# Layer 0 of a two-layer Fourier attention kernel: another opening, and transforms of 128 columns

## The chip, the cores and the metric

The kernel runs on one core of a Trainium2 chip. The core has a matrix engine (TensorE, PE in the profile, with its weight loads as PEld), VectorE (DVE), ScalarE (ACT), GpSimd (POOL) and SyncE (SP), which here only issues transfers. Each engine works through its own instructions in order and waits on semaphores for the others. The metric is the device time of one execution in microseconds, and lower is better. Everything is float32.

## The reference, cut to what matters

The input is four batches of 32 images of 128x128. Layer 0 normalises them (per group of image columns, then per image) and takes a Fourier transform of each image, of which 64 row and 33 column frequencies ("modes") are kept. Three sets of spectral weights make keys, queries and values for 32 heads. Attention runs over the 32 images of a batch, head by head, and the result is projected back. Two more spectral layers with a GELU between them follow, with a residual:

```python
xn = _inorm(xa, norm1_w, norm1_b)
k = _fno_layer(xn, Kcw, Ksw, Hs, Ws)
q = _fno_layer(xn, Qcw, Qsw, Hs, Ws)
v = _fno_layer(xn, Vcw, Vsw, H, W)
...
scores = jnp.einsum('bntk,bnsk->bnts', qf, kf) / (np.float32(np.sqrt(Hs * Ws)) * temperature)
p_attn = jax.nn.softmax(scores, axis=-1)
...
m = _fno_layer(an, m0cw, m0sw, H, W, inner_norm=True, act=True)
m = _fno_layer(m, m1cw, m1sw, H, W, inner_norm=True, act=False)
out = _inorm(m, mon_w, mon_b) + a
```

Layer 1 is an additive attention over the tokens and a mixture of experts. The change does not touch it.

## The kernel before

The kernel never forms keys, queries or values as images. All of it is done on modes. A mode is a pair of frequencies; with real and imaginary part, 64 row frequencies fill the 128 partitions.

A Tile scheduler sets the order of each engine's instructions from the program's order and its own estimates of time, and puts in the semaphores. A tile with the same tag and one buffer (`bufs=1`) reuses its memory, so a new writer waits for the last reader of the old contents. Pools of PSUM tiles have two buffers per tag.

**Loads.** `load(b)` (L113) brings a batch of images in as four transfers of 512 KB, two on SP's queue and two on ScalarE's. Then constants come on SP's queue (`cst`, `icol`, `par`). The spectral weights of the two later layers (`mcw_raw`, `mcol`, L153 to L159), `hs`, `pv` and `psw2` (L194 to L201) come as thirteen small transfers on ScalarE's queue. `mcw_raw` has one buffer for two sets, so the second set's transfer waits until VectorE has copied the first. ScalarE's table of functions is loaded in `logarithms()` (L299), which stands behind them.

**Statistics.** `image_sums` (L314) squares the images on ScalarE (L320), sums images and squares over rows with TensorE (`rows`, L324), copies the sums out (`ev`, L332) and turns them (`s12`, L337). A chain of small operations on VectorE, ScalarE and TensorE follows: `sv`, `mg`, `gm`, `gn_r` (the reciprocal deviation of a group), `colg` (the column transform scaled by it), `my`, `n_r` and `n_s` (the scale of each image).

**Key and query weights.** `padded` (L394) loads a weight with heads on 32 partitions, pads it from 32 to 64 row frequencies and makes its first column symmetric. For K and Q the kernel then multiplies on 32 partitions (L429 to L435), and brings the products to modes on partitions with 34 transposes on TensorE (L441). `w_re` and `w_im` are the result.

**Images' spectra.** `spectra_of_images` (L459) calls `forward` (L266) for groups of eight images. `forward` multiplies an image by `rows`, 192 columns wide: cosine, negative sine, negative cosine (`pz`, L274, two images to a PSUM tile). `evacuate` copies it to `z`, two calls in three on ScalarE (L219), the third on VectorE (L221). Two matmuls an image (`px`, L281 and L282) take the first 128 and the last 128 columns of `z` as weights. The results go to `xx`. The later layers' `spectra(0, q)` and `spectra(1, gl)` call the same `forward`. After all groups `xx` is corrected in places and written to a DRAM scratch `xd` with two transfers (L487), from where `xb` is read back in broadcast form (L698).

**Value weights.** `value_weights` (L500) multiplies value and projection weights on 32 partitions, writes them to DRAM (`gd`) and reads them back in broadcast (`gb`). It is called after the images' spectra.

**Attention.** `attention_weights` (L524) forms products over pairs of images on VectorE (`pa`) and GpSimd (`pb`), contracts them with `w_re` and `w_im` on TensorE (`sp`), adds the skip path and takes the softmax. The probabilities go through DRAM (`prd`) to `pr`. In the loop over batches `xb` is copied (`xw`, L707), multiplied with `gb` (`u`, L713 and L715) and contracted with `pr` (`po`, L718). For batches 1 to 3 the same work of the next batch is spread into the batch before it.

In the loop, between the first layer's spectra and the GELU, stands a chain on VectorE: `sqx` (L810), `v_s` (L814), `r0`, `hq` (L828). `add_attention` (L770), 32 updates of `x` a batch, may run anywhere between the attention's scale and the end of the batch.

Of the kernel before, what the change touches and what calls it, by code (L numbers as in the profile page):

```python
# [7 lines left out]
F32 = mybir.dt.float32  # L8
# [5 lines left out]
P = 128  # L14
# [21 lines left out]
def _constants():  # L36

    w = np.arange(P)
    kx = np.concatenate([np.arange(32), np.arange(-32, 0)])
    ky = np.arange(KY)  # L40
    th = 2 * np.pi / P
    c, s = np.cos(th * np.outer(w, kx)), np.sin(th * np.outer(w, kx))
    rows = np.concatenate([c, -s, -c], 1)
    inv_rows = np.concatenate([c.T, -s.T], 0)
    angle = th * np.outer(w, ky)
    cc, cs = np.cos(angle), np.sin(angle)

    cols1 = np.concatenate([cc[:, 32:33], cs, cc, -cs], 1) / NPIX
    cols2 = np.concatenate([0 * cc[:, :1], -cc, cs, cc], 1) / NPIX
    twice = np.where(ky == 0, 1.0, 2.0)[:, None]  # L50
    re, im = twice * cc.T, -twice * cs.T
    inv_cols = np.concatenate([re, im], 0)
    p = np.arange(P)
    same = (p[:, None] % 32 == np.arange(32)[None, :]).astype(np.float64)
    block = (p[:, None] // 32 == np.arange(4)[None, :]).astype(np.float64)

    eye = np.eye(32)
    comb = np.zeros((4, 32, 3, 32))
    comb[0, :, 0], comb[3, :, 0] = eye, -eye
    comb[1, :, 1], comb[2, :, 1] = eye, eye  # L60
    comb[:, :, 2] = -comb[:, :, 0]
    halves = np.concatenate([np.eye(64), np.eye(64)], 0)

    group = (p[:, None] // 4 == p[None, :] // 4) / (4.0 * NPIX / C * T)
    of_group = p[:, None] // 4 == np.arange(32)[None, :]
    by_p = np.concatenate(
        [rows, inv_rows, cols1, cols2, same, block, comb.reshape(P, 96), halves, group, of_group / 4],
        1,
    )
    return by_p.astype(np.float32), inv_cols.astype(np.float32)  # L70
# [3 lines left out]
NCONST = 192 + 128 + 2 * NX + 32 + 4 + 96 + 64 + P + 32  # L74
# [30 lines left out]
def layer0(  # L105
    tc, x, kcw, qcw, vcw, pcw, m0cw, m1cw, mcol0, heads, small_row, by_p, inv_cols, dram, x1
# [12 lines left out]

    loaded = load(0)  # L120
# [12 lines left out]
    rows = columns(192)  # L133
# [17 lines left out]

    mcw, energy, cross = [], [], []
    for n, src in enumerate((m0cw, m1cw)):  # L153
        t = const.tile([P, KY, 2], F32, name=f"mcw{n}_raw", tag="mcw_raw")
        m = const.tile([P, 2], F32, name=f"mcol{n}")
        for half in range(2):
            rows_h = slice(half * KX, (half + 1) * KX)
            nc.scalar.dma_start(out=t[rows_h], in_=src)
            nc.scalar.dma_start(out=m[rows_h], in_=mcol0[n])  # L159
        w = const.tile([P, 2, KY], F32, name=f"mcw{n}")  # L160
        nc.vector.tensor_copy(w, t.rearrange("p y r -> p r y"))
        mcw.append(w)
        sq = const.tile([P, 2, KY], F32, name=f"msq{n}")
        nc.vector.tensor_mul(sq, w, w)
        en = const.tile([P, KY], F32, name=f"energy{n}")
        nc.vector.tensor_tensor(en, sq[:, 0], sq[:, 1], ALU.add)
        lone = const.tile([P, 1], F32, name=f"lone{n}")
        nc.vector.tensor_scalar(lone, en[:, 0:1], 0.5, None, ALU.mult)
        nc.vector.tensor_scalar(en, en, 2.0, None, ALU.mult)

        h = const.tile([P, 2], F32, name=f"hermitian{n}")
        nc.vector.tensor_tensor(h[:, 0:1], w[:, 0, 0:1], m[:, 0:1], ALU.add)
        nc.vector.tensor_tensor(h[:, 1:2], w[:, 1, 0:1], m[:, 1:2], ALU.subtract)
        nc.vector.tensor_scalar(h, h, 0.5, None, ALU.mult)
        cr = const.tile([P, KY], F32, name=f"cross{n}")
        nc.vector.tensor_scalar(cr, w[:, 0], 2.0, None, ALU.mult)
        nc.vector.tensor_copy(cr[:, 0:1], h[:, 0:1])
        nc.vector.tensor_mul(h, h, h)
        nc.vector.tensor_tensor(en[:, 0:1], h[:, 0:1], h[:, 1:2], ALU.add)
        for r in (0, 64):  # L180
            nc.vector.tensor_copy(en[r + 32 : r + 33, 0:1], lone[r + 32 : r + 33])
            for v in (en, cr):
                nc.vector.memset(v[r : r + 1, 0:1], 0.0)
        energy.append(en)
        cross.append(cr)


# [6 lines left out]
    nc.scalar.dma_start(out=hs, in_=heads)  # L194
    ks, qs, vs, psw = (hs[:, i : i + 1] for i in range(4))
    pv = const.tile([2 * NH, 1], F32, name="pv")
    nc.scalar.dma_start(out=pv[:NH], in_=heads[:, 2:3])
    nc.scalar.dma_start(out=pv[NH:], in_=heads[:, 2:3])
    psw2 = const.tile([2 * NH, 1], F32, name="psw2")
    nc.scalar.dma_start(out=psw2[:NH], in_=heads[:, 3:4])  # L200
    nc.scalar.dma_start(out=psw2[NH:], in_=heads[:, 3:4])  # L201
    nc.vector.tensor_mul(pv, pv, psw2)

# [11 lines left out]
    def evacuate(out, in_):  # L215

        flip[0] = (flip[0] + 1) % 3
        if flip[0]:
            nc.scalar.copy(out, in_)  # L219
        else:  # L220
            nc.vector.tensor_copy(out, in_)  # L221
# [44 lines left out]
    def forward(images, c1, c2, take, change=None):  # L266
# [4 lines left out]
        for k in range(0, GI, 2):  # L271
            pz = ps.tile([P, 2, 192], F32, name="pz", tag="a")
            for j in range(2):
                nc.tensor.matmul(pz[:, j], images[k + j], rows, start=True, stop=True)  # L274
            evacuate(z[:, k : k + 2], pz)
# [23 lines left out]
    def logarithms():  # L299
        tc.keep_in_program_order(nc.scalar.preload_act_table_set("natural_log_exp_and_others"))  # L300

    logarithms()
# [86 lines left out]
    normed = image_sums(0, loaded)  # L389

# [3 lines left out]
    def padded(src, name, tag):  # L394
        raw = prep.tile([NH, 32, KA, 2], F32, name=f"{name}_raw", tag="raw", bufs=2)
# [17 lines left out]

    k_re, k_im = padded(kcw, "k", "k")
    q_re, q_im = padded(qcw, "q", "q")
    nc.vector.tensor_scalar(k_re, k_re, ks, None, ALU.add)
    nc.vector.tensor_scalar(q_re, q_re, qs, None, ALU.add)


    t1 = prep.tile([NH, KX, KA], F32, name="t1")  # L420
    t2 = prep.tile([NH, KX, KA], F32, name="t2")
    wd = prep.tile([NH, KA, 2, KX], F32, name="wd", tag="wd")
    for part, (a, b, c, d, op) in enumerate(
        (
            (q_re, k_re, q_im, k_im, ALU.add),
            (q_im, k_re, q_re, k_im, ALU.subtract),
        )
    ):
        nc.vector.tensor_mul(t1, a, b)  # L429
        nc.vector.tensor_mul(t2, c, d)  # L430
        nc.vector.tensor_tensor(t1, t1, t2, op)
        for half in range(2):
            view = wd[:, :, half, :].rearrange("n y x -> n x y")
            nc.vector.tensor_scalar(view, t1, 128.0, None, ALU.mult)
        nc.vector.tensor_scalar(wd[:, 0], wd[:, 0], 0.5, None, ALU.mult)  # L435
        dst = (w_re, w_im)[part]
        for y0 in range(0, KA, 16):
            n = min(16, KA - y0)
            pt = ps.tile([P, 16, NH], F32, name="pt", tag="a")
            for y in range(n):  # L440
                nc.tensor.transpose(  # L441
                    pt[:, y, :],
                    wd[:, y0 + y].rearrange("n h x -> n (h x)"),
                    ident[:NH, :NH],
                )
            nc.vector.tensor_copy(dst[:, y0 : y0 + n], pt[:, :n])

    nc.vector.memset(w_re[96:97, 0], 0.0)
    qk1 = prep.tile([NH, 1], F32, name="qk1")
    nc.vector.tensor_scalar(qk1, qs, ks, 128.0, ALU.mult, ALU.mult)  # L450
    qkd = prep.tile([NH, NH], F32, name="qkd")
    nc.vector.tensor_scalar(qkd, ident[:NH, :NH], qk1, None, ALU.mult)
    ones_n = prep.tile([NH, NH], F32, name="ones_n")
    nc.vector.memset(ones_n, 1.0)
    pq = ps.tile([NH, NH], F32, name="pq", tag="a")
    nc.tensor.matmul(pq, ones_n, qkd, start=True, stop=True)
    nc.vector.tensor_copy(qk, pq)

    def spectra_of_images(b, xt, normed):  # L459
# [4 lines left out]
        xx = modes.tile([P, T, n], F32, name=f"xx_{b}", tag="xx")  # L464
        for g in GROUPS:
# [12 lines left out]


        nc.vector.tensor_copy(xx[0:1, :, 1 + KY], par[0:1, N1B : N1B + 1].to_broadcast([1, T]))  # L480
        nc.vector.tensor_copy(xx[64:65, :, 1], par[64:65, N1B : N1B + 1].to_broadcast([1, T]))
# [3 lines left out]
        xd = dram.tile([T, 2, KX, KY], F32, name=f"xd_{b}")  # L485
        for part in range(2):
            nc.sync.dma_start(  # L487
                out=xd[:, part].rearrange("t x y -> x t y"),
                in_=xx[64 * part : 64 * part + 64, :, 1 + KY :],
            )  # L490
# [9 lines left out]
    def value_weights():  # L500

# [116 lines left out]

    front = spectra_of_images(0, loaded, normed)
    value_weights()  # L620
# [861 lines left out]
```

## Time and profile before

| | us |
|---|---|
| median of 3 runs (lowest, highest) | 3248.1 (3234.64, 3252.51) |
| the profiled execution | 3246.97 |
| its span | 3245.1 |
| PE, DVE, ACT, POOL busy | 3004.3, 2324.5, 2327.1, 2138.9 |
| granted TensorE clock, mean | 0.967 |

Some points of time in the profiled execution, from the timeline, for batch 0: the first `rows` matmul starts at 6.19 and the first square at 20.61; `gn_r` is done at 42.4 and `n_s` at 56.4; the copies `xm` of the finished spectra start at 76.26; the first product `pa` starts at 79.44; the first `po` starts at 125.61; `py`, which follows the last `po`, starts at 193.77.

The views: the *page* gives busy time and the costliest groups of instructions, with the idle time just before them and what ended most of it. The *chain of waits* follows the work that ended last back to what released each step. The *timeline* lists instructions in order. *Stretches* give the busy time of each engine between two moments. A float32 matmul appears as two records in the trace, so 256 records of `pz` are 128 images.

### The profile page before, as it was taken

How to read it: one execution, taken by the hardware profiler on the slowest of the kernel's cores; microseconds unless marked ns; L12 is line 12 of the kernel's file. 1: busy time of each engine (PE TensorE's matmuls, PEld its weight loads, DVE VectorE, ACT ScalarE, POOL GpSimd, SP SyncE). 2: the span in 40 equal slices, each digit the busy share in tenths (PEclk: the TensorE clock that was granted, in tenths of full speed). 3: DMA queues.
4: the chain of work that ended last, by engine and by line, in shares of the span. 5: the costliest groups of instructions: out<-in, count | busy, mean ns of one | idle time of the engine just before them, and what ended most of it. 6: DMA issues, size and time to landing. Idle time of an engine off the chain costs nothing.

```text
span 3245.1 us, 53386 instructions
## 1 busy us (share of the span) xinstructions
PE 3004.3 (93%) x19732; PEld 1584.7 (49%) x19732; DVE 2324.5 (72%) x5070; ACT 2327.1 (72%) x3205; POOL 2138.9 (66%) x1883
## 2 busy tenths in 40 slices
PE   6899899899898789999999999999999999999997
PEld 4378458548657734443444444444444435444443
DVE  6776767777686456777765868876677777687787
ACT  2244344354353469999998999998999999899992
POOL 1631551460461259978789887979878889888773
PEclk9899899999999779999999999999999999999999
DMA  4410420340230121010110010011100010101000
GB/s 107 111 32 1 100 70 1 50 121 1 29 116 1 44 55 30 1 37 7 25 42 23 1 36 14 8 30 30 30 14 24 14 36 24 36 1 30 14 14 13
DMA packets 150853, 111.67 MB, mean 34 GB/s; under 512 B 35870, under 2 KB 139393, under 8 KB 149985
## 3 DMA queue, kind: packets, MB, share of 16 engines
q1 hardware_dynamic: 133873, 102.42, 12.6%
q10 hardware_dynamic: 16720, 5.84, 0.8%
q8 instruction: 156, 2.56, 0.3%
q14 instruction: 104, 0.85, 0.1%
HBM read 67.26 MB, written 20.00 MB: 27 GB/s over the span
## 4 chain that ended last, share of the span: by engine, by line
PE 65%; POOL 10%; ACT 9%; DVE 8%; issue 6%; DMA 2%; ACTq 0%; POOLq 0%; DVEq 0%; SPq 0%
PE d L1293 19%; PE po L1312 11%; PE px L1181 6%; ACT r L1346 4%; PE po L718 4%; PE pz L274 4%; PE n L1293 4%; PE four L296 3%; POOL e L1355 3%; PE pv L291 3%; PE px L282 2%; PE px L281 2%; POOL e L1354 2%; ACT e L1362 2%; PE sk L682 1%
## 5 line engine op out<-in xcount | busy, mean ns | idle before, releaser
L1351 DVE TENSOR_TENSOR r<-n,r 128x1024 f32<-128x1024 f32 (+1 forms) x1056 | 961.4, 952 | 481.9 <-PE n L1293 388.5
L1354 POOL TENSOR_TENSOR e<-r 128x512 f32<-128x512 f32 x528 | 673.2, 1275 | 269.2 <-DVE r L1351 268.9
L1346 ACT ACTIVATE r<-d 128x1024 f32<-128x1024 f32 (+1 forms) x1056 | 793.0, 802 | 66.7 <-PE n L1293 59.9
L1358 ACT ACTIVATE r<-r 128x1536 f32<-128x1536 f32 x528 | 783.5, 1484 | 16.7
L1355 POOL TENSOR_TENSOR e<-e,r 128x512 f32<-128x512 f32 x528 | 671.5, 1272 | 41.4
L1293 PE MATMUL d<-qe,ke 32*128 32x512 f32 (+3 forms) x2304 | 611.0, 605 | 38.2 <-ACT r L1346 36.3
L1293 PE MATMUL n<-qe,ke 32*128 32x512 f32 (+3 forms) x2304 | 608.4, 603 | 0.0
L1312 PE MATMUL po<-e,kx 128*128 128x512 f32 (+3 forms) x1152 | 594.7, 605 | 13.4 <-POOL e L1367 13.4
L1293 PE MATMUL d<-qf,kf 32*128 32x512 f32 (+3 forms) x2304 | 555.2, 556 | 0.0
L1293 PE MATMUL n<-qf,kf 32*128 32x512 f32 (+3 forms) x2304 | 555.0, 556 | 0.0
L1185 DVE SCALAR_TENSOR_TENSOR xc<-px,wgt,xc 128x128 f32<-128x128 f32 x1024 | 358.1, 350 | 40.5 <-PE px L1181 9.5
L1362 ACT ACTIVATE e<-e 128x512 f32<-128x512 f32 x528 | 325.7, 617 | 64.4 <-POOL e L1355 63.7
L1312 PEld LDWEIGHTS po<-e,kx 128*128 128x128 f32 x1152 | 175.7, 188 | 392.2 <-issue 310.2
L1293 PEld LDWEIGHTS d<-qe,ke 32*128 32x128 f32 x2304 | 177.6, 184 | 360.1 <-ACT r L1346 340.8
L800 POOL TENSOR_TENSOR spec<-spec,part 128x264 f32<-128x264 f32 x64 | 55.5, 867 | 392.7 <-DVE part L797 188.9
L713 POOL TENSOR_TENSOR u<-xb,gb 128x858 f32<-128x858 f32 (+1 forms) x120 | 234.7, 1981 | 119.0 <-PE po L718 102.5
L1293 PEld LDWEIGHTS d<-qf,kf 32*128 32x128 f32 x2304 | 221.8, 187 | 177.1 <-issue 164.5
L1181 PE MATMUL px<-we,x2t 128*128 128x512 f32 x512 | 264.9, 603 | 6.8 <-DVE xc L1185 6.0
L715 DVE TENSOR_TENSOR u<-xw,gb 128x858 f32<-128x858 f32 (+1 forms) x200 | 206.6, 1084 | 51.1 <-PE po L718 37.1
L1293 PEld LDWEIGHTS n<-qf,kf 32*128 32x128 f32 x2304 | 229.0, 186 | 20.0 <-issue 12.4
L718 PE MATMUL po<-u,pr 128*32 128x429 f32 (+1 forms) x1280 | 188.6, 542 | 18.4 <-POOL u L713 8.8
L1293 PEld LDWEIGHTS n<-qe,ke 32*128 32x128 f32 x2304 | 178.0, 183 | 9.8 <-DVE r L1351 0.9
(369 smaller groups left out, 4254.4 us busy)
## 6 DMA issues: line engine op xcount, KB each, us to landing
xb<-xd SPq DMA_DIRECT2D x128, 214.5 KB
xc<-x SPq DMA_DIRECT2D x31, 512.0 KB
x<-x SPq DMA_DIRECT2D x16, 512.0 KB
qf<-qe SPq DMA_DIRECT2D x64, 128.0 KB
out<-xc SPq DMA_DIRECT2D x15, 512.0 KB
xb<-xd SPq DMA_DIRECT2D x32, 198.0 KB
gb<-gd SPq DMA_DIRECT2D x4, 1056.0 KB
x<-in_x ACTq DMA_DIRECT2D x8, 512.0 KB
```

Source lines behind the costliest of these rows:

```text
L713: nc.gpsimd.tensor_tensor(u, xb, gk, ALU.mult)
L718: nc.tensor.matmul(po[32 * j : 32 * j + 32], pr[:, i, k], u[:, r], start=i == 0 and k == 0, stop=i == 3 and k == 1,)
L1181: nc.tensor.matmul(px, x2t[:, k * P : (k + 1) * P], we[:, e0 : e0 + 4], start=True, stop=True)
L1185: nc.vector.scalar_tensor_tensor(xc[:, k], px[:, e], wgt[:, k, e0 + e : e0 + e + 1], xc[:, k], ALU.mult, ALU.add)
L1293: nc.tensor.matmul(o, k, q, start=turn == 0 or g > 0, stop=turn == 1 or g > 0)
L1312: nc.tensor.matmul(sums[c, h][:, q0 : q0 + c1 - c0], kx[:, jb], e[:, c0:c1], start=jb == 0, stop=is_last and q0 > 2 * P, skip_group_check= ...
L1346: nc.scalar.activation(r[:, g], d, AF.Ln, scale=1.0 / DSCALE)
L1351: nc.vector.tensor_tensor(r[:, g], part, r[:, g], ALU.mult)
L1354: nc.gpsimd.tensor_tensor(e, r[:, 1], r[:, 2], ALU.add)
L1355: nc.gpsimd.tensor_tensor(e, e, r[:, 0], ALU.add)
L1358: nc.scalar.activation(r, r, AF.Exp, scale=-1.0)
L1362: nc.scalar.activation(e, e, AF.Exp)
```

## The change

It has six parts.

- The table load (`logarithms()`) moves to the front, before `load(0)`. All small loads move from ScalarE's queue to SP's, and those of the later layers' weights, with the VectorE work on them, behind the key and query weights.
- `value_weights()` is called first, before `image_sums`. Its temporaries `t1`, `t2` are its own, and `padded` has one buffer for the raw weight instead of two.
- Key and query weights are laid out by the host with modes on partitions (`kq_modes`, `kq_mirror`, `heads_row`). They are loaded to both halves of the partitions and multiplied there as 128x544, without padding and without transposes.
- `rows` has 128 columns, without the negative cosine. `pz` holds four images, and the third block of `z` is made by a second evacuation with the sign changed.
- `evacuate` takes a sign: `activation(Copy, scale)` on ScalarE instead of `copy`, `tensor_scalar` on VectorE instead of `tensor_copy`, for all its callers.
- The bias of `xx` and the write to `xd` are done for each group of eight images, two small copies and two transfers of 66 KB each time.

```diff
-    rows = np.concatenate([c, -s, -c], 1)
+    rows = np.concatenate([c, -s], 1)
...
+    logarithms()
     loaded = load(0)
...
-    rows = columns(192)
+    rows = columns(128)
...
-            nc.scalar.dma_start(out=t[rows_h], in_=src)
-            nc.scalar.dma_start(out=m[rows_h], in_=mcol0[n])
...
-    nc.scalar.dma_start(out=hs, in_=heads)
+    nc.sync.dma_start(out=hs, in_=heads)
...
-    def evacuate(out, in_):
+    def evacuate(out, in_, sign=1.0):
         flip[0] = (flip[0] + 1) % 3
         if flip[0]:
-            nc.scalar.copy(out, in_)
+            nc.scalar.activation(out, in_, AF.Copy, scale=sign)
         else:
-            nc.vector.tensor_copy(out, in_)
+            nc.vector.tensor_scalar(out, in_, sign, None, ALU.mult)
...
-        for k in range(0, GI, 2):
-            pz = ps.tile([P, 2, 192], F32, name="pz", tag="a")
-            for j in range(2):
+        for k in range(0, GI, 4):
+            pz = ps.tile([P, 4, P], F32, name="pz", tag="a")
+            for j in range(4):
                 nc.tensor.matmul(pz[:, j], images[k + j], rows, start=True, stop=True)
-            evacuate(z[:, k : k + 2], pz)
+            evacuate(z[:, k : k + 4, :P], pz)
+            evacuate(z[:, k : k + 4, P:], pz[:, :, :64], -1.0)
...
-    k_re, k_im = padded(kcw, "k", "k")
-    q_re, q_im = padded(qcw, "q", "q")
...
-            for y in range(n):
-                nc.tensor.transpose(
-                    pt[:, y, :],
-                    wd[:, y0 + y].rearrange("n h x -> n (h x)"),
-                    ident[:NH, :NH],
-                )
-            nc.vector.tensor_copy(dst[:, y0 : y0 + n], pt[:, :n])
...
+            for r, y in ((0, 1 + KY), (64, 1)):
+                bias = par[r : r + 1, N1B : N1B + 1].to_broadcast([1, GI])
+                nc.vector.tensor_copy(xx[r : r + 1, i, y], bias)
+            for part in range(2):
+                nc.sync.dma_start(
+                    out=xd[i, part].rearrange("t x y -> x t y"),
+                    in_=xx[64 * part : 64 * part + 64, i, 1 + KY :],
+                )
...
+    value_weights()
+    normed = image_sums(0, loaded)
     front = spectra_of_images(0, loaded, normed)
-    value_weights()
...
+    nc.sync.dma_start(out=skip, in_=heads_row[: 2 * NH].partition_broadcast(P))
...
+        for h in range(2):
+            r = slice(64 * h, 64 * h + 64)
+            nc.sync.dma_start(out=raw[r], in_=kq_modes[n])
+            nc.sync.dma_start(out=rev[r], in_=kq_mirror[n])
...
+    for dst, a, c, op in (
+        (w_re, q_re, q_im, ALU.add),
+        (w_im, q_im, q_re, ALU.subtract),
+    ):
+        t = prep.tile(shape, F32, name="wt", tag="wt")
+        nc.vector.scalar_tensor_tensor(dst, a, 128.0, k_re, ALU.mult, ALU.mult)
+        nc.vector.scalar_tensor_tensor(t, c, 128.0, k_im, ALU.mult, ALU.mult)
+        nc.vector.tensor_tensor(dst, dst, t, op)
+        nc.vector.tensor_scalar(dst[:, 0], dst[:, 0], 0.5, None, ALU.mult)
...
+            nc.sync.dma_start(out=t[rows_h], in_=src)
+            nc.sync.dma_start(out=m[rows_h], in_=mcol0[n])
```

## The prediction

> **What bounds the kernel now.** I read the span first: 3245.1 us, inside an execution of 3246.97. Layer 1 begins at about 1128 us and the change does not touch it, so some 2117 us stay. Then the chain of waits over the first 130 us. Columns: start us, us, what.
>
> ```profile
> 4.91 7.48 DMA mcw_raw<-in_m0cw
> 13.35 6.09 DMA mcw_raw<-in_m1cw
> ...
> 35.65 1.19 DVE t L431
> ...
> 76.98 15.32 DMA xd<-xx
> 92.32 16.41 DMA xb<-xd
> ```
>
> Two tiny loads hold the first 19 us, VectorE's K/Q products on 32 partitions hold 24 to 42, then the transforms, then a scratch write and its read-back up to 109. The timeline says how the tiny loads get there: they stand on ScalarE's queue ahead of its table load and the squares, and one of them waits for a buffer.
>
> ```profile
> 19.31 1.28 ACT L300 ACT_TABLE_LOAD   x1 [19.31 <-DMA mcw_raw<-in_m1cw]
> 20.61 1.06 ACT L320 ACTIVATE xx<-x 128x1024 f32<-128x1024 f32 x1
> ...
> 30.56 0.58 ACT L332 COPY ev<-rows 64x512 f32<-64x512 f32 x1 [6.06 <-PE rows L324]
> ```
>
> The image was there at 6.2 us (the first `rows` matmul runs at 6.19), the squares start at 20.61, the sums end at 30.5. Third, the groups, for the transforms of all four batches (busy, mean ns | idle before):
>
> ```profile
> L219 ACT COPY z<-pz 128x384 f32<-128x384 f32 x127 | 60.5, 477 | 120.2 <-PE pz L274 119.9
> L274 PE MATMUL pz<-cst,x 128*128 128x192 f32 x256 | 54.3, 354 | 4.0 <-ACT z L219 3.0 <-DVE z L221 1.0
> L282 PE MATMUL px<-colg,z 128*128 128x67 f32 x256 | 49.1, 275 | 0.0
> ```
>
> ScalarE waits for TensorE (120 us), TensorE hardly for ScalarE (3): these stages are bound by TensorE. `pz` alone is 3.9% of the whole chain, 127 us for 384 images: 0.33 us each.
>
> Last, busy time by stretch (PE, PEld, DVE, ACT, POOL, clock, DMA share, GB/s):
>
> ```profile
> 79.40:106.30 26.90, 25.70 (x138) 5.07 (x138) 25.16 (x23) 0.00 (x0) 21.84 (x12) 0.87 0.72 117
> ...
> 218.00:247.00 29.00, 25.98 (x194) 24.60 (x192) 26.27 (x91) 7.74 (x22) 6.55 (x8) 1.00 0.01 1
> ...
> 300.00:332.00 32.00, 31.32 (x243) 29.95 (x242) 17.02 (x49) 7.21 (x18) 2.43 (x2) 1.00 0.01 1
> ```
>
> The attention of batch 0 (first row) is VectorE's, the first layer's spectra (second) are TensorE's with VectorE as full, the second layer's spectra with the next batch's images (third) are TensorE's alone.
>
> **The opening, as far as the sums.** Thirteen small loads leave ScalarE's queue and the table load goes to the front. It then costs 1.28 us before ScalarE issues its half of the image, instead of 18 us before the squares. The image and the constants (2.4 MB) had landed by about 11.5 us (the load of `par`, waiting for a piece of the image, goes out at 11.79). The last square (1.05) then ends near 12.7, and two pairs of `rows` (0.85 at full clock) near 14.5, against 30.5: **-16 us**.
>
> [...] `rows` steps take 0.85 us from 21.71 and 0.43 from 25.64. In the new order TensorE is idle twice (before `colg`, before `n_s`, below)[...].
>
> **From the sums to the spectra.** In the new order VectorE does the value weights in the middle of the statistics. From `sv` (16.4) to `gn_r`: about 1.5 us of small operations and two waits for TensorE (0.9 each); two `z` evacuations, 0.68 and 0.41 (from 0.55 for 384 columns and 0.68 for 512); `p1` 0.77; eight products and sums of 32x1088 at 1.27 (row of L513), less the last one, 9; corrections 1. That gives `gn_r` near 31, `colg` 32 against 43.2. On to `n_s`: one more product 1.27; seven K/Q operations of 128x544, which the trace lacks: 0.65 each, half of the 1.21 of 128x1024 (L559); below 0.3 there is no row, above 1.27 neither, so 2 to 9 us, I take 4.5; two evacuations 1.1; small operations 4. **`n_s` is ready near 43.5, against 56.4.** What leaves: K and Q on 32 partitions (4 x 1.08, 6 x 1.27, 2 x 0.77, 4 evacuations) and 34 transposes.
>
> After `n_s`, 24 images of `px` at 0.447 (two of 0.223, from starts at 50.96 and 51.63) make 10.7 us, the last group's `pz` lying before them; with the slow clock the spectra end near **57 against 76.1**. The first image stage did 18.8 us there.
>
> **Scratch write and read-back.** `xd` is now written in eight transfers of 66 KB. [...] the two took 15.32 us for 0.54 MB. Split, three groups lie beside the transforms and only the last, 15.3/4 = 4 us, comes after. I take the row. SP's order then is: second half of `gb`, `xd`, eight tiny loads, two pieces of image 1 (1 MB, formerly at 20 us), `xb`. From 46 us that is 2.1 + 0.5 + 1.0 + 0.4 MB to the first pair of `xb`; at the 117 GB/s of the attention row, 35 us: 81. It is needed at 89, where the scores end. So it is hidden by 8 us; today `xw` holds `spt` from 106.3 to 109.26, which goes too. Image 1 is wanted first at 189, so its delay is free.
>
> **Attention to the first `po`.** 57 + 3.3 (copies) + 26.9 (that row) + 2 (the second `mcw` set, 13 operations of 0.15, now among the products) = 89. From `spt` to the first `po`, 16.3 us today (109.26 to 125.6); I take 16: **105 against 125.6, -21 us.** Range -12 to -27.
>
> **Transforms of 128 columns.** `pz` loses the third block: 0.326 becomes 0.223 (the pace of `four`, L296, with 128 columns, and of `px`), 0.103 an image. The negated block is now a second evacuation: on ScalarE 0.58 for 512 columns (spt) + 0.38 for 256 (0.8 ns a column below 0.477), 0.96 for four images, against 2 x 0.477; nothing. The write as ACTIVATE instead of COPY: 0.59 to 0.62 in rows of 512, at most 0.05 more, under cover of 75% idle. `evacuate` of `v` and `yf` likewise.
> - Second layer's spectra and images, batches 0 to 2: 64 images x 0.103 = 6.6, with fewer stops (blocks of four in two PSUM buffers) 7: **-21**. VectorE 17 of 32 busy: cover enough. What follows (POOL's `pb`) just starts earlier. Batch 3, 32 images: **-3.5**.
> - First layer's spectra, four times: TensorE -3.3 and its waits -1, but VectorE is as full. In the built order 12, 7, 10 and 12 of the 32 updates `x` (L770, spaced 0.29) now stand behind `sqx`, inside the chain to `hq`; today none. That chain has gaps (0.67, 2.13, 0.56 us), so of 3.5 us some 2 show. Net -2 to -3 each: **-9.5** (ends -2 and -17).
> - The split bias copies: 8 instead of 2 a batch, 0.19 each, beside TensorE; nothing.
>
> **Sum:** -21 - 21 - 3.5 - 9.5 = -55 from 3246.97: 3192. The median of the runs shown is 1 us above that execution, so **3193 us**.
>
> **Rivals.**
> - Hand-over takes the transforms' gain (18%): where both evacuations of a block fall to ScalarE (about 1.0 with latency) TensorE's 0.89 a block waits, and VectorE holds the first layer's spectra. For it: VectorE 26.27 of 29. Against: ScalarE 7.2 of 32. Opening -21, transforms -8: 3219.
> - The opening gains only a third (12%): value weights ahead of `gn_r` run on, or `xb` lands after the scores. `gn_r` 7 us later and `xb` 7 us late leave -7: 3207.
> - No cover needed (6%): the updates fit in the gaps (-17), no slow clock (-24), -24.5 elsewhere: 3182.
> - **Slower** (2%): 132-byte rows of `xd`, now mixed with `gb`, image 1 and `xb`, drag all of it to their own pace, 0.54 MB in 15.3 us = 35 GB/s. Then 4.0 MB from 46 us end at 160, `po` begins at 176, +51; with the transforms' -34: 3264. It decides from about 45 GB/s down, where the loss passes 34. [...]
> - The change is not what it says (2%, about 3245): the built order shows `pz` at 128 columns and the table load first.
>
> **How the numbers follow.** The forecast's own case has 60%, with 3178 to 3206. With the first two rivals (3219, 3207) and the third (3182) 96% is named; the range goes to the first of them and a little past it, and below to the unmeasured K/Q operations and updates at their low ends: **3171 to 3221**. A measurement here can tell about 0.5% (16 us) from no change. Faster by more: 95%; within: 3%; slower: 2%.
>
> **What would show it.** The squares start near 6 and `rows` ends before 16; `n_s` near 43; `xm` near 57; first `po` near 105. `pz` at 128x128 has a pace of 0.223 and idle before it stays under 5 us a kind. First `sqx` to `hq` grows from 7.8 to about 10 us. Layer 1 keeps its length within 5 us. The forecast is wrong if `gn_r` waits for the values beyond 36, if `xw` still waits for `xb` after the scores, or if idle before `pz` grows to tens of us.

## The result, and the profile after

| | before | after |
|---|---|---|
| median of the runs, us | 3248.1 (3234.64 to 3252.51) | 3214.38 (3212.99 to 3215.65) |
| after / before | | 0.9903, 95% interval 0.9874 to 0.9932 |
| profiled execution, its span | 3246.97, 3245.1 | 3214.14, 3212.4 |

It became faster by 1.0%, 34 us where I had forecast 55. The head of the page of the kernel after:

```profile
span 3212.4 us, 53393 instructions
## 1 busy us (share of the span) xinstructions
PE 2971.1 (92%) x19698; PEld 1558.3 (49%) x19698; DVE 2317.7 (72%) x5072; ACT 2323.7 (72%) x3205; POOL 2134.2 (66%) x1879
```

TensorE was busy for 3004.3 us before: its own work shrank by 33. The first part of the opening went as the change says. ScalarE's timeline, after (start us, us, engine, line, what [idle before <- what ended it]):

```profile
0.78 1.28 ACT L121 ACT_TABLE_LOAD   x1 [0.78 <-PEq L1467]
...
6.11 2.00 ACT L277 ACTIVATE xx<-x 128x1024 f32<-128x1024 f32 x2 [4.05 <-DMA x<-in_x]
10.12 1.06 ACT L277 ACTIVATE xx<-x 128x1024 f32<-128x1024 f32 x1 [2.00 <-DMA x<-in_x]
12.91 1.06 ACT L277 ACTIVATE xx<-x 128x1024 f32<-128x1024 f32 x1 [1.73 <-DMA x<-in_x]
...
16.77 0.58 ACT L289 COPY ev<-rows 64x512 f32<-64x512 f32 x1 [2.81 <-PE rows L281]
```

The squares start at 6.11 instead of 20.61, and `ev` stands at 16.77 instead of 30.56. Of these 13.8 us, 7.6 are left at the first `po` (117.96 instead of 125.61). VectorE's timeline in the scores of batch 0, after:

```profile
71.14 3.47 DVE L473 TENSOR_TENSOR pa<-xp,xm 128x1024 f32<-128x1024 f32 x3
75.07 1.22 DVE L473 TENSOR_TENSOR pb<-xp,xm 128x1024 f32<-128x1024 f32 x1 [0.46 <-PE sp L479]
76.21 3.48 DVE L473 TENSOR_TENSOR pa<-xp,xm 128x1024 f32<-128x1024 f32 x3
82.23 0.29 DVE L591 COPY mcw<-mcw_raw 128x66 f32<-128x66 f32 x1 [2.54 <-DMA mcw_raw<-in_m1cw]
```

The scores start at 71.1 instead of the forecast 60.3, and among them VectorE, which works in order, stops for a 16.5 KB load: spectral weights of the second later layer (`in_m1cw`; with its `mcol` below called the second set). The transforms, by group (busy, mean ns | idle before):

```profile
L178 ACT ACTIVATE z<-pz 128x512 f32<-128x512 f32 x63 | 37.5, 595 | 82.2 <-PE pz L233 62.5 <-PE px L243 18.4 <-issue 1.3
L233 PE MATMUL pz<-cst,x 128*128 128x128 f32 x256 | 36.5, 292 | 7.2 <-ACT z L178 7.0
```

The image transforms of four batches fell from 54.3 us busy to 36.5, and TensorE waits 7.2 us for a `z` instead of 4.0. And the stretches, after, that answer to those of before: the scores, the first layer's spectra, the second layer's with the next images (PE, PEld, DVE, ACT, POOL, clock, DMA share, GB/s):

```profile
71.10:102.00 30.90, 26.51 (x130) 4.74 (x130) 27.66 (x42) 0.00 (x0) 21.27 (x12) 0.79 0.46 113
...
211.00:240.00 29.00, 25.33 (x205) 24.20 (x204) 24.69 (x84) 7.40 (x22) 6.99 (x8) 0.96 0.01 1
284.00:316.00 32.00, 29.95 (x258) 28.93 (x257) 20.17 (x65) 7.65 (x21) 3.74 (x4) 1.00 0.18 41
```

In 29 us TensorE now does 205 matmul records where it did 194, and 258 in 32 us where it did 243. The scores take 30.9 us instead of 26.9.

Laid out by stage, from the starts of the same instructions in both traces (in brackets the time within the stage at a granted clock of 0.50). `spt` is ScalarE's copy of the contracted products `sp`, with which the work on pairs of images ends:

| stage | before | after | forecast | measured |
|---|---|---|---|---|
| up to the first `py` | 193.8 (41) | 186.9 (65) | -21 | -6.8 |
| `py` to `hq`, four batches | 238.6 (19) | 234.0 (24) | -9.5 | -4.6 |
| `hq` to the next `xm`, three | 235.4 (4) | 220.5 (10) | -21 | -14.9 |
| `xm` to `spt`, three | 106.6 (31) | 110.5 (34) | 0 | +4.0 |
| `spt` to `py`, three | 267.6 (7) | 268.0 (10) | 0 | +0.3 |
| last `hq` to layer 1's first score | 117.9 (70) | 106.7 (56) | -3.5 | -11.2 |
| from there to the end | 2085.3 | 2085.9 | 0 | +0.6 |

So 14 us of the 22 that are missing were lost in the opening, 6 in the second layer's transforms and 5 in the first layer's; 4 more went into the later scores; the tail gave 8 too many.

### The profile page after: what moved, and what is told of

Its sections match the earlier page's. It is cut to its first block, busy times and chain, and to the rows that moved or that the text cites. A ratio compares the mean times of both kernels' runs of the same rounds, so it can differ in the third digit from the quotient of the medians.

```text
span 3212.4 us, 53393 instructions
## 1 busy us (share of the span) xinstructions
PE 2971.1 (92%) x19698; PEld 1558.3 (49%) x19698; DVE 2317.7 (72%) x5072; ACT 2323.7 (72%) x3205; POOL 2134.2 (66%) x1879
## 4 chain that ended last, share of the span: by engine, by line
PE 59%; POOL 11%; ACT 8%; DVE 7%; issue 5%; DMA 0%; POOLq 0%; DVEq 0%; ACTq 0%; SPq 0%
PE d L1297 19%; PE po L1316 11%; PE px L1185 6%; ACT r L1350 4%; PE n L1297 4%; PE po L722 3%; POOL e L1359 3%; POOL e L1358 3%; PE four L257 2%; PE pv L252 2%; PE px L243 2%; PE px L242 2%; POOL kx L1050 1%; ACT e L1366 1%; PE pz L233 1%
## 5 line engine op out<-in xcount | busy, mean ns | idle before, releaser
L1362 ACT ACTIVATE r<-r 128x1536 f32<-128x1536 f32 x528 | 783.5, 1484 | 16.7
L1359 POOL TENSOR_TENSOR e<-e,r 128x512 f32<-128x512 f32 x528 | 671.2, 1271 | 41.4
L1297 PE MATMUL d<-qe,ke 32*128 32x512 f32 (+3 forms) x2304 | 610.0, 604 | 38.3 <-ACT r L1350 36.5
L1366 ACT ACTIVATE e<-e 128x512 f32<-128x512 f32 x528 | 325.6, 617 | 65.1 <-POOL e L1359 64.3
```

What stands on the lines that cost most here:

```text
L1297: nc.tensor.matmul(o, k, q, start=turn == 0 or g > 0, stop=turn == 1 or g > 0)
L1359: nc.gpsimd.tensor_tensor(e, e, r[:, 0], ALU.add)
L1362: nc.scalar.activation(r, r, AF.Exp, scale=-1.0)
L1366: nc.scalar.activation(e, e, AF.Exp)
```

## Experiments

The opening in all kernels, in us, from their timelines. "Wait" is VectorE's idle time, among the scores, before an operation that waits for a load of the two later layers' weights.

| kernel | `xm` | wait | `spt` | first `po` | ratio to before, 95% |
|---|---|---|---|---|---|
| before | 76.3 | none | 109.3 | 125.6 | |
| after | 67.9 | 2.5 | 103.7 | 118.0 | 0.9903, 0.9874 to 0.9932 |
| fill_both | 63.5 | 13.2 | 110.1 | 124.3 | 0.9937, 0.9917 to 0.9957 |
| fill_512 | 60.7 | 9.3 | 102.5 | 116.7 | 0.9909, 0.9893 to 0.9924 |
| fill_67 | 64.8 | 6.1 | 103.4 | 119.0 | 0.9913, 0.9896 to 0.9930 |
| t128_alone | 74.3 | none | 119.2 | 136.2 | 0.9964, 0.9949 to 0.9980 |
| loads_away | 66.1 | none | 96.5 | 111.0 | 0.9906, 0.9881 to 0.9931 |
| loads_away_512 | 62.0 | none | 91.8 | 106.3 | 0.9872, 0.9848 to 0.9895 |
| loads_away_both | 64.3 | none | 94.8 | 109.3 | 0.9896, 0.9861 to 0.9931 |
| values_after | 62.4 | 5.9 | 103.1 | 117.3 | 0.9912, 0.9887 to 0.9937 |
| pool_pb_first | 57.8 | 12.4 | 102.7 | 116.9 | 0.9814, 0.9791 to 0.9836 |
| opening_alone | 60.6 | 12.3 | 108.9 | 123.2 | 0.9982, 0.9972 to 0.9993 |
| xd_in_two | 61.1 | none | 91.4 | 105.9 | 0.9863, 0.9838 to 0.9887 |
| three_edits | 60.8 | none | 91.1 | 105.6 | 0.9792, 0.9769 to 0.9815 |

### Is it the clock?

My first theory came from one row of the kernel after: the 24 images of `px` behind `n_s`. For it I made two runs with extra matmuls in the same place, of 512 columns in one and of 67 in the other, and a third that fills both idle stretches. The row, a stretch of the kernel after (columns as above):

```profile
46.50:67.00 20.50, 20.50 (x96) 20.49 (x96) 6.12 (x35) 1.25 (x3) 0.00 (x0) 0.50 0.53 112
```

TensorE is busy for all 20.5 us, and the clock stays at 0.50. A record of `px` starts every 0.214 us instead of the 0.112 that it takes at 1.00 (a matmul is two records), an image takes 0.85 instead of 0.45, and the 24 images take 9.7 us longer.

```diff
 forward(... scaled, less_mean)
+if b == 0 and g == 2 * GI:
+    extra = ps.tile([P, 512], F32, name="extra", tag="wide")
+    for j in range(6):
+        nc.tensor.matmul(extra, xt[:, j], xt[:, 4:8], start=True, stop=True)
```

That is fill_512. fill_67 has 24 of them with `cst[:, :67]` in place of `xt[:, 4:8]`; fill_both has 12 of 512 columns behind group 1 (of 0 to 3) and 10 behind group 2 (I had meant 6), in a tile of tag "a".

> The changed kernel with 12 matmuls of 128x512 on TensorE in its idle stretch before bg and 6 more before the wait for n_s; they write a PSUM tile that nobody reads. Clock theory (the opening lost its gain because the granted clock stood at 0.50 from 29 to 77 us): the clock stays at 1.00 through px, 24 images of px take 10.7 us instead of 20.4, xm is at about 58 instead of 67.9, first po near 108 instead of 118, the time near 3204. Rival (VectorE or the loads set this stretch anyway): xm moves by under 3 us, the time stays within 3211 to 3216.

> The changed kernel with 6 matmuls of 128x512 (5.1 us at half rate) ahead of the last pz blocks, in the half-rate stretch itself. Theory[...]: the clock is back at 1.00 by about 50, px takes 0.223 a matmul, xm near 60, the time near 3207. Rival (it is the time busy that counts, or something outside this stretch): still 0.50 up to 75, xm at 73, the time near 3219.

> The same place and the same 5.1 us of TensorE, but 24 matmuls of 67 columns instead of 6 of 512. Theory[...]: no return of the clock, 0.50 up to about 76, px 0.427 a matmul, xm near 73, the time near 3219. Rival (busy time counts): the same as with 512 columns.

The stretch 45 to 52, first of fill_512, then of fill_67:

```profile
45.00:52.00 7.00, 7.00 (x48) 5.57 (x48) 2.67 (x14) 0.00 (x0) 0.00 (x0) 1.00 0.56 117
```

```profile
45.00:52.00 7.00, 7.00 (x34) 7.00 (x34) 2.40 (x12) 0.00 (x0) 0.00 (x0) 0.50 0.59 126
```

In both TensorE is busy throughout, for 7.00 of 7.00 us. With 512 columns the clock was back at 44.8 (by about 50 was expected); with 67 it stayed at 0.50 through 10.2 us of extra matmuls (twice what I had meant, for I had counted one record for each) and came back at 52.7, behind a run of `pz`, where I had expected no return before 76. Width and number of the extra matmuls differ together, so what in them brought the clock back is not shown. But what I had built on the clock fell: in fill_512 `xm` is 7.2 us earlier than after, and the first `po` 1.2. VectorE's timeline of fill_512 says where the 6 us went:

```profile
69.05 3.47 DVE L479 TENSOR_TENSOR pa<-xp,xm 128x1024 f32<-128x1024 f32 x3
81.81 0.20 DVE L597 COPY mcw<-mcw_raw 128x66 f32<-128x66 f32 x1 [9.29 <-DMA mcw_raw<-in_m1cw]
```

The copy waits until 81.8, as it did at 82.2 in the kernel after, whatever the clock did. fill_both, which kept the clock at 1.00 up to 66.8, came out slower than after: its copy also had to wait until 81.1, and the built order had put it behind one product instead of seven, so more of them stood behind it.

pool_pb_first (below) has the opening of the kernel after, instruction by instruction, and no extra matmuls; there the clock came back at 45.8 by itself and `xm` is 10 us earlier. Its VectorE:

```profile
66.13 3.48 DVE L473 TENSOR_TENSOR pa<-xp,xm 128x1024 f32<-128x1024 f32 x3
82.01 0.20 DVE L591 COPY mcw<-mcw_raw 128x66 f32<-128x66 f32 x1 [12.40 <-DMA mcw_raw<-in_m1cw]
```

First `po` 116.9 against 118.0. `xm` plus wait is 70.4, 70.0, 70.9 and 70.2 us in after, fill_512, fill_67 and pool_pb_first: the wait takes whatever the clock gives. In these four, seven of VectorE's 22 products stand before the wait; with one (fill_both) the sum is 76.7, with five (opening_alone) 72.9, with nine (values_after) 68.3.

### The loads behind gb

What the copy waits for is on SyncE's queue. Its timeline, after:

```profile
53.83 1.24 SPq L433 DMA_DIRECT2D gb<-gd  x2
55.18 21.61 SPq L396 DMA_DIRECT2D xd<-xx  x6
76.83 0.64 SPq L588 DMA_DIRECT2D mcw_raw<-in_m1cw  x1
```

The second half of `gb` (2.1 MB) goes out at 53.8; the six `xd` behind it then take 21.6 us. For 4.6 us SyncE waits for the third group's spectra; two of the six hold the queue for 7.1 and 7.2 us each where the others take 0.6, the last of these two until 76.1, just after `gb`'s last packet (75.8). Only then does the 16.5 KB load go out. The one buffer that both sets share does not hold it: VectorE had copied the first set at 44.4.

```diff
-t = const.tile([P, KY, 2], F32, name=f"mcw{n}_raw", tag="mcw_raw")
+t = const.tile([P, KY, 2], F32, name=f"mcw{n}_raw", tag=f"mcw{n}_raw")
 ...
-    nc.sync.dma_start(out=t[rows_h], in_=src)
+    (nc.gpsimd if n else nc.sync).dma_start(out=t[rows_h], in_=src)
 ...
-nc.sync.dma_start(out=pv[:NH], in_=heads[:, 2:3])
+nc.gpsimd.dma_start(out=pv[:NH], in_=heads[:, 2:3])
```

The loads of `mcol`, of the other half of `pv` and of `psw2` change likewise. loads_away_512 has the 6 wide matmuls besides, loads_away_both 12 behind group 1 and 4 behind group 2.

> The changed kernel with eight small loads of layer 0's opening on GpSimd's queue instead of SyncE's: the second mode-mixer set (mcw_raw and mcol of in_m1cw, which get a raw tile of their own) and pv and psw. Theory (in the opening VectorE's scores wait for these loads, which stand behind the second half of gb and the eight xd on SyncE's queue until 82 us): the 2.54 us wait goes, VectorE's 13 operations on the set move out of the scores, spt at about 99 to 101 instead of 103.66, the clock as before, the time near 3211. Rival (the stall is small and hidden, the clock alone sets the opening): spt stays at 103 to 104, the time at 3214.

> The same with the 6 matmuls of 128x512 that brought the clock back early. Theory (clock and load are two walls, one behind the other; either alone gives 1 to 3 us, both together the 10 that were missing): xm at 60.7, spt near 91, first po near 105, the time near 3203. Rival (a third wall stands there, xb, which comes behind the same gb): spt near 91, but first po at 110 or later, the time 3207 to 3211.

> The loads away, and TensorE never idle long: 12 matmuls of 128x512 before bg, 4 before the wait for n_s. Theory: the clock stays at 1.00 up to the scores, xm near 57 as I had forecast, spt near 88, first po near 104, the time near 3202. If xb is the next wall: xm 57, but first po no earlier than in the run with 6 matmuls.

VectorE's timeline of loads_away_512, in which nothing of the kind stands between the products any more:

```profile
74.27 3.46 DVE L479 TENSOR_TENSOR pa<-xp,xm 128x1024 f32<-128x1024 f32 x3
77.66 1.20 DVE L479 TENSOR_TENSOR pb<-xp,xm 128x1024 f32<-128x1024 f32 x1
78.79 3.46 DVE L479 TENSOR_TENSOR pa<-xp,xm 128x1024 f32<-128x1024 f32 x3
```

The two walls stand one behind the other. The clock alone gave 1.2 us at the first `po`; the loads alone 7.0 (at `spt` 7.1, where I expected 3 to 5: with the 2.5 us wait, the set's 13 operations and the stops of TensorE went, and `xm` came 1.8 earlier); both together 11.7, and the first `po` stands at 106.3 where my forecast had 105. `xb` is no third wall here: ScalarE's first `xw`, at 90.25, is released by VectorE, and the packets of the first `xb` are through at 87.4. That leaves 3 us. loads_away_both missed: its clock fell to 0.50 at 47.8, at the start of the long run of `px`, and stayed there to 75 (see the last section). The time of loads_away, 3216.2, does not show its 7 us; in its profiled execution later stages of layer 0 ran longer at 0.50 than in the kernel after (mean granted clock 0.960 against 0.963; what that costs, in the part on the halves).

```diff
-value_weights()
 normed = image_sums(0, loaded)
+value_weights()
```

> The changed kernel with the value weights' instructions behind the image sums instead of ahead of them, nothing else. Theory (gb's 4.2 MB hold SyncE's queue for 46 us and all that stands behind them is late by as much as gb is): gn_r near 23 and xm below 60, no idle stretch of 6 us and the clock at 1.00, but gb starts 8 to 10 us later, the wait for the second mixer set ends at about 90, and first po is no earlier than 118: 3214 or more. Rival (VectorE's value weights ahead of gn_r and the clock cost the opening): first po near 108, 3204.

The first `po` came at 117.3, near the 118 of the theory, but not for the whole of its reason: `gb` went out 1.6 us later, not 8 to 10 (the first half at 32.8 instead of 31.2), and the wait ended at 83.0. The clock fell as well: it stood at 0.50 from 32.2 to 73.2. The rival, first `po` at 108, is out: to put the value weights first is no mistake, and no gain that shows, while the set stands behind `gb`.

xd_in_two is loads_away_512 with `xd` in two transfers:

```diff
-            for part in range(2):
-                nc.sync.dma_start(out=xd[i, part]..., in_=xx[..., i, 1 + KY :])
+        for part in range(2):
+            nc.sync.dma_start(out=xd[:, part]..., in_=xx[..., 1 + KY :])
```

> The run loads_away_512 with xd in two transfers behind the last group instead of eight. My forecast's step (split, three quarters of the 15.3 us lie beside other work): xb lands 7 to 11 us later, first po at 112 to 117 instead of 106, the time near 3210. Queue theory in its strong form (xd waits for gb in either case, the split gains nothing): first po within 2 us of 106, the time near 3204.

First `po` at 105.9, 0.4 us from the run with eight. My step is refuted: in both runs the first packet of `xb` starts at 85.9. Its SyncE:

```profile
54.56 1.21 SPq L438 DMA_DIRECT2D gb<-gd  x2
61.05 14.72 SPq L405 DMA_DIRECT2D xd<-xx  x2
```

Eight or two, the last of them goes out when `gb` is through, at about 76 (75.8 in this timeline). That is the strong form of the queue theory, with one limit: `xd`'s last packet ends at 83.7 with two and at 80.7 with eight, and `xb` is level because one 512 KB piece of the next image, which stood between `xd` and `xb`, now goes out ahead of `gb`'s second half, at 41.4. So the split is worth 3 us at the end of `xd`, and nothing at `xb`. At the first `py` xd_in_two is 1.1 us ahead; the 6 us between the medians arise in later batches, in stages with more time at 0.50 (`spt` to `py` of batch 2, 96.4 us with 13.7 of it, against 90.6 with 3.4). The edit holds for all batches, so a part of its own in them is not excluded.

### Each half of the change alone

t128_alone is the kernel before with `evacuate` and `forward` of the change; opening_alone is the change with these two, and the third block of `rows`, as before. The core of the first:

```diff
-    pz = ps.tile([P, 2, 192], F32, name="pz", tag="a")
+    pz = ps.tile([P, 4, P], F32, name="pz", tag="a")
 ...
-    evacuate(z[:, k : k + 2], pz)
+    evacuate(z[:, k : k + 4, :P], pz)
+    evacuate(z[:, k : k + 4, P:], pz[:, :, :64], -1.0)
```

> The kernel before with the transforms of 128 columns alone; its opening as it was. My forecast had -34 for this part: 3214. From the change's own trace (all of it -33, its opening -7) about -26: 3221. Hand-over theory (evacuations take the gain): -8, 3239.

> The changed opening with transforms of 192 columns as before. Theory: first po about where the change has it (118, 7.6 us ahead of before), since gb and the load behind it set it and not the transforms; nothing gained behind it: the time near 3239. If the transforms' width sets the opening too[...]: xm well ahead of 67, first po 113 to 116.

The halves alone give 0.36% and 0.18%; together they give 1.0%. t128_alone, 3235.57 us, is far from my forecast (3214) and near the hand-over theory's 3239, but not for that theory's reason: behind the first `py` its span is 23.2 us shorter than that of before, and up to there 11.6 us are lost. ScalarE, t128_alone:

```profile
117.15 0.52 ACT L709 COPY xw<-xb 128x429 f32<-128x429 f32 x1 [39.85 <-DMA xb<-xd]
```

There `xw` waits for `xb` until 117 (before: 107.7), and `spt` stands behind it. In the old order the value weights come behind the spectra; with shorter transforms the second `gd` went out at 83.8, behind `xd`, instead of at 68.5, and the second half of `gb` at 93.4 instead of 82.7. So the change's opening is worth 18.2 us at the first `po` with the short transforms (136.2 to 118.0) and 2.4 with the long ones (125.6 to 123.2): each half repairs what the other alone would spoil. In opening_alone `xm` came at 60.6, as its second theory had it, but the first `po` at 123.2, later than either theory's (118, or 113 to 116): VectorE waited 12.3 us for a load of `mcol` behind the same `gb`, and was through with the scores no earlier.

The halves also show how far the clock moves a stage. `py` to `hq` with 192 columns takes 58.5 to 60.0 us, with 128 columns 57.1 with no time at 0.50, 57.1 to 58.7 with 3.4 us of it, and 58.3 to 61.2 with 10.2: by my estimate up to half a microsecond for each at 0.50 (1.6 us for 3.4, 4.1 for 10.2). The tail of batch 3, 117.9 before, takes 110.2 in opening_alone, with the old transforms (51 us at 0.50 instead of 70; VectorE and GpSimd do the same operations in the same order, and TensorE is busy for 75.0 us instead of 85.1). So most of the 11.2 us that it gained, some 8 by my estimate (117.9 less 110.2), are the clock's.

### GpSimd in the later scores

The table of stages has `xm` to `spt` 4.0 us longer, with nothing changed there. GpSimd's timeline of batch 2, after:

```profile
581.44 2.35 POOL L900 TENSOR_TENSOR x<-x,g 128x1024 f32<-128x1024 f32 x1 [28.47 <-ACT g L893]
583.76 3.77 POOL L475 TENSOR_TENSOR pb<-xm 128x1024 f32<-128x1024 f32 x2
587.49 2.36 POOL L900 TENSOR_TENSOR x<-x,g 128x1024 f32<-128x1024 f32 x1
589.82 1.90 POOL L475 TENSOR_TENSOR pb<-xm 128x1024 f32<-128x1024 f32 x1
...
595.87 2.35 POOL L900 TENSOR_TENSOR x<-x,g 128x1024 f32<-128x1024 f32 x1
```

Four updates of `x`, which nobody waits for yet, stand between the products `pb`, for which TensorE waits. In the kernel before two of the four fell into this stretch of batch 2, which took 33.9 us and now takes 37.7. In batches 1 and 3 as many stand there in both kernels, four and three.

```diff
-nc.gpsimd.tensor_tensor(xr[:, i], xr[:, i], gl[:, i], ALU.add)
+with tc.issue_after(last_pb):      # batches 0 to 2: the last pb on GpSimd
+    nc.gpsimd.tensor_tensor(xr[:, i], xr[:, i], gl[:, i], ALU.add)
```

> The changed kernel with GpSimd's four updates of x (L900) in batches 0 to 2 issued behind the last pb of the next batch's scores, nothing else. Theory (with shorter transforms xm comes while these updates still stand ahead of pb on GpSimd, 2.35 us each, which took back 4 us of the transforms' gain): xm to spt takes 34 to 35 us in all three later batches instead of 38.4, 37.7 and 34.4, the updates' readers on VectorE are not late, the time near 3208. Rival (what the scores gain the last stage loses, since it waits for x): xm to spt shorter, spt to py longer by as much, 3214.

It did more than expected: `xm` to `spt` takes 29.9, 30.2 and 30.4 us, 20 less in three batches, and `spt` to `py` stays at 268.3 in all (268.0 after). The group of TensorE's matmuls from `pb`, 150 to 1050 us, in before, after and pool_pb_first:

```profile
L565 PE MATMUL sp<-pb,w_im 128*32 128x512 f32 x204 | 61.0, 712 | 19.0 <-POOL pb L561 18.6
```

```profile
L479 PE MATMUL sp<-pb,w_im 128*32 128x512 f32 x204 | 62.2, 722 | 23.3 <-POOL pb L475 23.0
```

```profile
L479 PE MATMUL sp<-pb,w_im 128*32 128x512 f32 x204 | 58.3, 671 | 2.4 <-POOL pb L475 1.7
```

The waiting was there before the change (18.6 us), the change added 4.4, and the new order takes nearly all of it away.

> Loads away, 6 matmuls of 128x512, and pb ahead of the updates of x, together. If the three walls are separate: first po near 106, xm to spt 34 to 35 in the later batches, the time near 3198. If the last edit only moves the wait: 3204.

3187.55 us median (3183.64 to 3189.79), 0.9792 of before: it beats both kernels. It came out below what I expected because the last edit was worth 20 us in its stages (16 in the medians, against loads_away_512) and not 5.

## Why the prediction was right, and where its sum was not

The direction and the range held; the sum was 22 us too large. By its own steps:

- **Opening as far as the sums, -16.** Held to 2 us: `rows` ended at 16.7 instead of 14.5, since the last quarter of the image landed at 12.9 and not by 11.5.
- **From the sums to `n_s`, 43.5.** Held: 45.3. `gn_r` at 32.0 (31), the 128x544 operations 0.72 us (0.65). No stall for the values.
- **"with the slow clock the spectra end near 57".** Mis-sized. Of the 13.5 us from `n_s` to there `px` had 10.7, so some 3 were left for the last `pz` and the slow clock. The clock stood at 0.50 from 29.3 to 77.1; 24 images of `px` took 20.4 us instead of 10.7, and `xm` came at 67.9 instead of 57. From 46.5 to 67.0 TensorE was busy without a gap, 20.5 us, at 0.50 throughout.
- **"+ 2 (the second `mcw` set, 13 operations of 0.15, now among the products)".** This is the step that failed. I priced the set's operations and not the load in front of them, and of SyncE's order I asked only when `xb` would land. The load stands behind the same `gb` and `xd`; VectorE, in order, waits for it until 82, and with the clock repaired still until 81.8. With the loads elsewhere and the clock back the first `po` is at 106.3, as forecast (105): the rest of the opening's arithmetic was sound.
- **`xb` hidden by 8 us.** Right for the kernel after, but by luck: the first `xb` is through at 88.8 and not at 81, and the scores end at 103.7 and not at 89. In loads_away_512, where they end at 91.8, it is hidden by 3.
- **Split of `xd`: "only the last, 15.3/4 = 4 us, comes after".** Wrong as a reason. In eight pieces half of `xd`, not three quarters, went before `gb` was through, and it ended 3 us sooner than in two; xd_in_two has the same first `po`. The row of `xd` alone did not decide on this queue, which a larger transfer, `gb`'s second half (2.1 MB), filled until about 76.
- **Transforms, second layer, -21.** 14.9, of which most is explained: where the clock stayed at 1.00, `hq` to `xm` took 70.2 and 71.1 for batch 1 (pool_pb_first, fill_512; 79.3 before, 3.9 of it at 0.50) and 72.3 for batch 3 (77.1 before); batch 2 gave only 2.5, with 6.8 us at 0.50 where there had been none, and 2.5 us more of TensorE's idle time. The hand-over rival was right in small: 1 to 3 us a batch.
- **"What follows (POOL's `pb`) just starts earlier".** Wrong: +4.0 in three batches, since GpSimd still had its updates to do.
- **First layer's spectra, -9.5.** -4.6. The first sum of `sqx` to `hq` grew from 7.8 to 9.6 us, as forecast (10); about -2 a batch at equal clock, +0.9 in batch 3 with 10.2 us at 0.50.
- **Batch 3's tail, -3.5.** -11.2, some 8 of it the clock's. That error hid a part of the others.
- **Evacuations at nothing.** Held: 0.595 and 0.379 us on ScalarE (0.58 and 0.38); its idle time before them is 107 us, TensorE's wait for them at the images 7.

Of the rivals the one nearest to the result was "the opening gains only a third" (-7); its number was right and its reason, a late `gn_r` or a late `xb`, was not.

## What to carry to other kernels

When a stage moves forward, list every load that an in-order engine waits for in that stretch, the tiny ones for later use too, and find what each stands behind on its queue: price the load, not the operations that read it. Look for work without a deadline on an in-order engine between the operations of a critical stage; the profile shows it as idle time of the consumer, here 18.6 us released by `pb`, of which a changed order left 1.7. Compare stages and not totals for an edit of some 5 us, since the same stage of the same code differed by up to 4 us from kernel to kernel with its time at a granted clock of 0.50 (`py` to `hq` with 128 columns: 57.1 us with none of it, up to 61.2 with 10.2).

## What was not expected of the hardware

**The same run of `px` came at two clocks.** after, loads_away and pool_pb_first run the same TensorE instructions as far as `px`, and have `xm` at 67.9, 66.1 and 57.8. Stretches within the run of `px`:

| stretch, us | kernel | PE busy, us | matmul records | clock |
|---|---|---|---|---|
| 46.5 to 57.0 | pool_pb_first | 10.50 of 10.50 | 95 | 1.00 |
| 46.5 to 67.0 | after | 20.50 of 20.50 | 96 | 0.50 |
| 47.8 to 64.0 | loads_away_both | 16.06 of 16.20 | 77 | 0.50 |

TensorE was busy throughout, or nearly, in all three rows, so its busy time within the run does not part them. Ahead of it, loads_away_both had TensorE busy for 11.22 of the 12 us from 34 to 46, at 1.00, and its clock fell at 47.8; in pool_pb_first the clock came back at 45.8, and `px` ran at 1.00. What decides which of the two a run gets is not shown. `xm` of after and of pool_pb_first differ by 10.1 us.

**A transfer's neighbours on the queue outweighed its own size here.** A load of 16.5 KB that is issued in 0.64 us went out at 76.8, 48 us behind its twin of the first set (29.1), for standing behind `gb`; and the write of 0.54 MB let the first `po` start within 0.4 us of the same time in two pieces and in eight (105.9 and 106.3).
